# A state-space scan loop: two of sixteen blocks take their input through ScalarE and GpSimd, and the steps around the loop are placed anew

## The chip, the core and the metric

The kernel runs on one core of one Trainium2 chip. The metric is the time of one execution in microseconds of device time. The kernel before took 2898.57 us, the median of three runs (2897.48 to 2911.18). The profile shown in this document is of one further execution, which took 2914.13 us and whose profiled span is 2912.3 us.

## What is computed

The reference is a two-layer model on a tensor of 4 images, 256 channels and 32 x 32 pixels (1024 positions). Layer 0 holds four small state-space blocks ("mamba"), one for each group of 64 channels, then gates, depthwise convolutions, attention and a projection. Layer 1 is a second attention and a mixture of 16 experts. The change lies wholly in the state-space part, which for one image and one channel group is this:

```python
u = silu(causal_conv(u))                       # 128 inner channels, 1024 positions
dt = softplus(xdbc[..., :4] @ dtw.T + dtb)     # 128 x 1024
Bm, Cm = xdbc[..., 4:20], xdbc[..., 20:]       # 16 states, 1024 positions each
def selective_scan(u, dt, Bm, Cm, A, Dp):
    dA = exp(dt[..., None] * A)
    dBu = (dt * u)[..., None] * Bm[:, :, None, :]
    def step(h, inp):
        dA_t, dBu_t, C_t = inp
        h = dA_t * h + dBu_t
        return (h, einsum('bds,bs->bd', h, C_t))
    ...
    return ys + u * Dp
y = selective_scan(...) * silu(z) @ outw.T
```

## The kernel before

**Tiles.** An image and a channel group make one *group* `n` of the loop: 16 groups, image by image (`order`, four of them an image). A group has 128 inner channels with 16 states each, 2048 recurrences along 1024 positions. They are cut into `NJ` = 16 *blocks* of 8 channels x 16 states = 128 partitions x 1024 positions. The loop runs over `t` = 0 to 255 (`NBLK`) blocks; `n, j = t // 16, t % 16`. Every tile named below is 128 x 1024 float32.

**One block** is made by five engines:

- the DMA queue of SyncE (`fetch`, L869) spreads the 8 rows of `dt` over 128 partitions into `dA` (five buffers), and ScalarE (`decay`, L874) takes the exponential in place;
- TensorE (`select`, L881) multiplies a 0/1 matrix `pick` with `U`, three bfloat16 parts of dt*u, so that PSUM tile `dBu` (two buffers) holds dt*u on 128 partitions;
- VectorE multiplies `dBu` in PSUM by `B` (L940) and runs the recurrence `h = dA*h + dBu` (L943) into `hs` (six buffers);
- GpSimd multiplies `hs` by `C` (L944);
- TensorE sums over the states into `pY` (`add_up`, L892 for the first block and the last two, L899 for pairs of the others) and adds u * D (L905). `pY` has one buffer.

**The order of the work** is written out by hand: each engine works through its own queue in the order in which the loop body emits. Iteration `t` emits the multiply and the scan of block `t`, the C-multiply of `t`, `select(t + 2)`, `add_up(t - 3)`, `fetch(t + 4)`, `decay(t + 3)`, and then *front* steps of the coming group, which make its `u`, `dt`, `U`, `B` and `C`. The list at L526 to L529 gives each front step the `j` at which it is emitted (negative numbers are in the group before):

| step | engines and lines | j before | j after |
|---|---|---|---|
| `project(0..3)`, the convolution | TensorE L464 | -5, -4, -3, -2 | -4, -3, -3, -1 |
| `silu` | ScalarE L468 | -1 | -1 |
| `project_dt` | TensorE L475 | 0 | 0 |
| `exps` | ScalarE L480 to L483, four operations | 1 | 0 |
| `rest` | VectorE L486, GpSimd L487 | 3 | 3 |
| `log` | ScalarE L490 | 4 | 3 |
| `dt_out` | VectorE L493, DMA L495, GpSimd L496 | 5 | 5 |
| `part1`, `part2`, the bfloat16 parts | ScalarE L500, L505; GpSimd L501, L506 | 6, 7 | 6, 7 |
| `spread(0)`, `spread(1)`, B and C | TensorE L522, ScalarE L524 | 6, 7 | 6, 9 |
| `parts_out`, `turn` | DMA L510, L517 | 10, 12 | 11, 12 |

Behind the loop steps of the group just finished are emitted too: `gated` (ScalarE copies `pY` into `u`, L546), `times_gate` (GpSimd, L549, j = 4), `project_out` (TensorE, L559 and L560), `store` (ScalarE, L565), `gate` of the running group (TensorE L537, ScalarE L539), `module_gate` (TensorE L578 or L589, j = 5, in groups 5, 6, 7, 9, 10, 11, 13, 14, 15) and `module` (GpSimd L594, in groups 6, 7, 10, 11, 14, 15). All products of front and back steps share one PSUM tile, `mm` (`big()`).

**What waits for what around the change.** `select` of a block needs its PSUM buffer back from the scan two blocks earlier. The first `add_up` of a group needs `pY` back, that is `gated` of the group before. `dt_out` on VectorE needs `log` of ScalarE and the subtraction L487 of GpSimd. The scan needs an `hs` buffer that `add_up` has read.

Of the kernel before, what the change touches and what calls it, by code (L numbers as in the profile page):

```python
# [10 lines left out]
F32 = mybir.dt.float32  # L11
BF16 = mybir.dt.bfloat16
AF = mybir.ActivationFunctionType
ALU = mybir.AluOpType
# [3 lines left out]
B, C, HH, WW = 4, 256, 32, 32  # L18
N = HH * WW
NP = N + 2  # L20
P = 128
CT = C // P
NT = N // P
NB, DM, DIN, DS, DTR, K = 4, 64, 128, 16, 4, 4
# [352 lines left out]
def body(tc, g, out):  # L377
    nc = tc.nc
    act, mm = nc.scalar.activation, nc.tensor.matmul
    ts, tt, stt = nc.vector.tensor_scalar, nc.vector.tensor_tensor, nc.vector.scalar_tensor_tensor  # L380
    HALVES = (slice(0, 512), slice(512, 1024))
# [5 lines left out]
    with pool("const", 1) as cp, pool("dram", 1, space=bass.MemoryType.DRAM) as drp, contextlib.ExitStack() as late:  # L387
# [46 lines left out]
        with pool("mconst", 1) as mc, pool("front", 1) as fp, pool("dts", 2, space=bass.MemoryType.DRAM) as dsp, pool(  # L434
# [17 lines left out]
            def front(n):  # L452


                nb, b = order[n]
                rows_in, xb = block(nb, b)
                r = state[n] = {}

                def project(part):
                    if part == 0:  # L460
                        r["pu"] = big()
                    h = HALVES[part // 2]
                    for k in range(part % 2 * 2, part % 2 * 2 + 2):
                        mm(r["pu"][:, h], m_cu[rows_in, nb // 2, k], xb[:, k + h.start : k + h.stop], start=k == 0, stop=k == K - 1)  # L464

                def silu():
                    r["u"] = fp.tile([P, N], F32, tag="u", name="u", bufs=3)
                    act(r["u"], r["pu"], AF.Silu, bias=V("convb", nb), scale=1.0)  # L468

                def project_dt():
                    r["pdt"] = big()
                    for h in HALVES:
                        mm(r["pdt"][:, h], m_wdt[:, nb, :], r["u"][:, h], start=True, stop=True)  # L475

                def exps():
                    e = r["e"] = fp.tile([P, N], F32, tag="e", name="e")
                    dt = r["dt"] = fp.tile([P, N], F32, tag="dt", name="dt")
                    act(e, r["pdt"], AF.Abs, bias=V("dtb", nb), scale=1.0)  # L480
                    act(dt, r["pdt"], AF.Relu, bias=V("dtb", nb), scale=1.0)
                    act(e, e, AF.Exp, scale=-1.0)
                    act(r["pdt"], e, AF.Identity, bias=one, scale=1.0)  # L483

                def rest():
                    stt(r["e"], r["pdt"], -1.0, r["e"], ALU.add, ALU.subtract)  # L486
                    nc.gpsimd.tensor_tensor(r["dt"], r["dt"], r["e"], ALU.subtract)  # L487

                def log():
                    act(r["pdt"], r["pdt"], AF.Ln)  # L490

                def dt_out():
                    tt(r["dt"], r["dt"], r["pdt"], ALU.add)  # L493
                    r["ds"] = dsp.tile([NJ, DB, N], F32, tag="ds", name="ds")
                    nc.sync.dma_start(out=r["ds"].rearrange("j d n -> (j d) n"), in_=r["dt"])  # L495
                    nc.gpsimd.tensor_tensor(r["e"], r["dt"], r["u"], ALU.mult)  # L496

                def part1():
                    p = r["parts"] = fp.tile([P, 3, N], BF16, tag="parts", name="parts")
                    nc.scalar.copy(p[:, 0], r["e"])  # L500
                    nc.gpsimd.tensor_tensor(r["e"], r["e"], p[:, 0], ALU.subtract)  # L501

                def part2():
                    p = r["parts"]
                    nc.scalar.copy(p[:, 1], r["e"])  # L505
                    nc.gpsimd.tensor_tensor(p[:, 2], r["e"], p[:, 1], ALU.subtract)  # L506

                def parts_out():
                    dq = r["dq"] = dsp.tile([P, 3, N], BF16, tag="dq", name="dq")
                    nc.sync.dma_start(out=dq, in_=r["parts"])  # L510

                def turn():

                    dq = r["dq"]
                    U = r["U"] = fp.tile([96, 4, N], BF16, tag="U", name="U", bufs=2)
                    for q in range(3):
                        nc.sync.dma_start(out=U[32 * q : 32 * q + 32], in_=dq.rearrange("(t c) q n -> q c t n", c=32)[q])  # L517

                def spread(c):
                    p = big()  # L520
                    for h in HALVES:
                        mm(p[:, h], m_bc[:, nb, c * P : (c + 1) * P], r["u"][:, h], start=True, stop=True)  # L522
                    t = r["BC"[c]] = fp.tile([P, N], F32, tag=f"bc{c}", name=f"bc{c}", bufs=2)
                    nc.scalar.copy(t, p)  # L524

                return [(i - 5, lambda i=i: project(i)) for i in range(4)] + [  # L526
                    (-1, silu), (0, project_dt), (1, exps), (3, rest), (4, log), (5, dt_out), (6, part1),
                    (6, lambda: spread(0)), (7, part2), (7, lambda: spread(1)), (10, parts_out), (12, turn),
                ]  # L529

            def gate(n):
# [66 lines left out]
            with pool("scan", 6) as sp, pool("yps", 1, space=PSUM) as yps, pool("dps", 2, space=PSUM) as dps, pool("lnA", 1) as wp:  # L598
# [8 lines left out]
                add, pre.spare, pre.slack, pre.split = pre.add, (2, 3), 700, True  # L607
                xs = [[sp.tile([P, N], F32, tag="hs", name="hs") for k in range(CT)] for b in range(B - 1)]
                for b in range(B - 1, B):
                    t = wp.tile([P, CT, N], F32, tag=f"xs{b}", name=f"xs{b}")  # L610
                    xs.append([t[:, k] for k in range(CT)])
                    late_gate.append(t.rearrange("p k n -> p (k n)")[:96, 0:NP])
                convr = sp.tile([P, N], F32, tag="dA", name="dA", bufs=5).rearrange("p (t k d) -> p t k d", t=CT, k=K)
                roots = [sp.tile([P, N], F32, tag="dA", name="dA", bufs=5) for b in range(2)]
                roots += [wp.tile([P, N], F32, tag="r", name="r")] * 2
# [241 lines left out]

                dAs, dBus, hss = {}, {}, {}  # L860

                def which(t):

# [7 lines left out]
                def decay(t):  # L871
                    if t < NBLK:
                        c = order[t // NJ][0] * NJ + which(t)
                        act(dAs[t], dAs[t], AF.Exp, scale=aneg[:, c : c + 1])  # L874

                def select(t):
                    if t < NBLK:
                        j = which(t)
                        dBus[t] = dps.tile([P, N], F32, tag="dBu", name="dBu")
                        for h in HALVES:  # L880
                            mm(dBus[t][:, h], pick[:, j % 4], state[t // NJ]["U"][:, j // 4, h], start=True, stop=True)  # L881

                def add_up(t):
                    if not 0 <= t < NBLK:
                        return
                    r, p, j = state[t // NJ], t % NJ, which(t)
                    if p == 0:
                        r["pY"] = yps.tile([P, N], F32, tag="y", name="pY")
                    if not 2 <= p < 14:
                        hs = hss.pop(t)  # L890
                        for h in HALVES:
                            mm(r["pY"][:, h], strip[:, P - DB - j * DB : 2 * P - DB - j * DB], hs[:, h], start=p == 0, stop=p == NJ - 1)  # L892
                    elif p % 2:

                        two = {which(u): hss.pop(u) for u in (t - 1, t)}
                        for h in HALVES:
                            for c, hs in two.items():
                                q, i = c // 4, c % 4
                                mm(  # L899
                                    r["pY"][32 * q : 32 * q + 32, h], strip[:, P - DB - i * DB : P - i * DB + 32 - DB], hs[:, h],  # L900
                                    start=False, stop=False,
                                )
                    if p in (0, 1):
                        h = HALVES[p]
                        mm(r["pY"][:, h], ddiag[:, order[t // NJ][0]], r["u"][:, h], start=False, stop=False)  # L905

                fronts = [front(n) for n in range(1, len(order))]
# [26 lines left out]
                with tc.manual_schedule():  # L934
                    for t in range(NBLK + 4):
                        n, j = t // NJ, t % NJ
                        if t < NBLK:
                            r = state[n]
                            dBu = dBus.pop(t)
                            tt(dBu, dBu, r["B"], ALU.mult)  # L940

                            hs = hss[t] = sp.tile([P, N], F32, tag="hs", name="hs")
                            nc.vector.tensor_tensor_scan(hs, dAs.pop(t), dBu, 0.0, ALU.mult, ALU.add)  # L943
                            nc.gpsimd.tensor_tensor(hs, hs, r["C"], ALU.mult)  # L944
                        if j == 3 and n > 0:
                            gated(n - 1)
                        select(t + 2)
                        add_up(t - 3)
# [11 lines left out]
                            times_gate(n - 1)  # L960
                        last = n == len(order)
                        for i in range(2):
                            if n > 0 and j == (3 if last else 8 + i):
                                project_out(n - 1, i)
                        if n > 0 and j == (3 if last else 9):
                            store(n - 1)
                        if not last and j == 10:
                            gate(n)
                        if n > NB and j == 5 and n % NB > 0:
                            module_gate(n // NB - 1, n % NB - 1)  # L970
                        if n > NB and j == 8 and n % NB > 1:
                            module(n // NB - 1, n % NB - 2)


# [1103 lines left out]
```

## Time and profile before

| what | value |
|---|---|
| median of three runs | 2898.57 us |
| the profiled execution | 2914.13 us |
| its span | 2912.3 us |
| scan loop, first to last scan (L943) | 102.7 to 1068.1 us |
| TensorE busy over the span | 89% |
| VectorE | 69% |
| ScalarE | 53% |
| GpSimd | 44% |
| TensorE clock granted, mean | 0.947 |

The page of a profile lists busy time by engine, forty equal slices of the span, DMA queues, the chain of work that ended last and the costliest groups of instructions: after the bar come busy time in all, the mean duration of one in ns, and the idle time of the engine just before them with what ended most of it. The timeline lists instructions in order of time: start and duration in us, engine, line, operation; identical neighbours are merged, and a bracket gives the idle time before the row and what released it. The windows view gives the busy time of every engine in a stretch and the clock granted to TensorE in it (1.00 is full speed).

### The profile page before, as it was taken

How to read it: one execution, taken by the hardware profiler on the slowest of the kernel's cores; microseconds unless marked ns; L12 is line 12 of the kernel's file. 1: busy time of each engine (PE TensorE's matmuls, PEld its weight loads, DVE VectorE, ACT ScalarE, POOL GpSimd, SP SyncE). 2: the span in 40 equal slices, each digit the busy share in tenths (PEclk: the TensorE clock that was granted, in tenths of full speed). 3: DMA queues.
4: the chain of work that ended last, by engine and by line, in shares of the span. 5: the costliest groups of instructions: out<-in, count | busy, mean ns of one | idle time of the engine just before them, and what ended most of it. 6: DMA issues, size and time to landing. Idle time of an engine off the chain costs nothing. (4 is left out here: it accounts for less than half of the span.)

```text
span 2912.3 us, 38753 instructions
## 1 busy us (share of the span) xinstructions
PE 2582.6 (89%) x15252; PEld 1505.6 (52%) x15252; DVE 1999.3 (69%) x2260; ACT 1554.3 (53%) x2097; POOL 1281.2 (44%) x806
## 2 busy tenths in 40 slices
PE   6788888888888779999899899989799997899996
PEld 3322222222222225666556556554566676799996
DVE  5799999999999986867876895783655465111112
ACT  3666666766766635766855875783433332111111
POOL 0587778877888850000010010101234235666662
PEclk7799999999999989999999999999899997999998
DMA  3467667776677641001000000000000003655445
GB/s 141 119 175 176 173 163 177 184 179 173 171 176 192 169 137 41 5 9 33 5 1 27 19 1 12 20 1 15 1 8 16 8 15 97 196 134 136 111 111 174
DMA packets 95433, 269.57 MB, mean 93 GB/s; under 512 B 18695, under 2 KB 36727, under 8 KB 91921
## 3 DMA queue, kind: packets, MB, share of 16 engines
q1 hardware_dynamic: 66560, 202.52, 26.5%
q0 software_dynamic: 26512, 60.35, 8.1%
q10 hardware_dynamic: 2176, 4.19, 0.4%
q8 instruction: 121, 1.98, 0.3%
q14 instruction: 64, 0.52, 0.1%
HBM read 291.57 MB, written 42.80 MB: 115 GB/s over the span
## 5 line engine op out<-in xcount | busy, mean ns | idle before, releaser
L944 POOL TENSOR_TENSOR hs<-hs,bc 128x1024 f32<-128x1024 f32 x256 | 600.9, 2356 | 162.1 <-DVE hs L943 157.2
L943 DVE TENSOR_TENSOR_SCAN hs<-dA,dBu 128x1024 f32<-128x1024 f32 x256 | 585.3, 2286 | 38.9 <-PE pY L899 10.0
L1286 DVE TENSOR_REDUCE nm<-s 128x1 f32<-128x1024 f32 x256 | 302.8, 1218 | 100.7 <-PE s L1277 99.8
L874 ACT ACTIVATE dA<-dA,aneg 128x1024 f32<-128x1024 f32 x256 | 286.3, 1144 | 105.9 <-DMA dA<-ds 104.0
L1291 ACT ACTIVATE pr<-s,nm 128x1024 f32<-128x1024 f32 x256 | 285.5, 1118 | 82.0 <-DVE nm L1286 44.4
L940 DVE TENSOR_TENSOR dBu<-dBu,bc 128x1024 f32<-128x1024 f32 x256 | 309.8, 1210 | 11.1 <-PE dBu L881 11.0
L1305 PE MATMUL k<-const,pr 128*128 128x128 f32 x2048 | 282.8, 280 | 31.1 <-ACT pr L1291 20.0
L1355 POOL TENSOR_TENSOR b<-b 128x1024 f32<-128x1024 f32 (+1 forms) x15 | 29.6, 1973 | 633.7 <-ACT b L1351 633.7
L1305 PEld LDWEIGHTS k<-const,pr 128*128 128x128 f32 x2048 | 227.7, 142 | 149.2 <-issue 76.3
L881 PE MATMUL dBu<-U,pick 96*128 96x512 bf16 x512 | 161.1, 397 | 121.4 <-DVE hs L943 121.2
L1953 PE MATMUL s<-pT,b 128*128 128x128 f32 x1920 | 236.4, 280 | 8.2 <-DMA b<-we,intse 6.9
L1953 PEld LDWEIGHTS s<-pT,b 128*128 128x128 f32 x1920 | 231.5, 196 | 14.3 <-issue 6.3
L899 PE MATMUL pY<-hs,const 128*32 128x512 f32 x768 | 214.6, 686 | 0.0
L1957 DVE TENSOR_TENSOR pT<-pT,s 128x512 f32<-128x512 f32 x72 | 49.3, 684 | 230.3 <-ACT pT L1956 230.3
L1309 ACT COPY pT<-k 128x512 f32<-128x512 f32 x299 | 165.2, 592 | 57.8 <-PE k L1305 56.4
L881 PEld LDWEIGHTS <-pick 96*128 96x128 bf16 x512 | 39.9, 98 | 298.0 <-issue 172.5
L1277 PE MATMUL s<-b,b 32*128 32x512 f32 x512 | 177.1, 652 | 8.1 <-ACT pr L1291 8.0
L1309 DVE COPY pT<-k 128x512 f32<-128x512 f32 x213 | 140.1, 684 | 62.3 <-PE k L1305 60.1
L1277 PE MATMUL s<-b,qs 32*128 32x512 f32 x512 | 177.1, 652 | 0.0
L1325 PE MATMUL k<-pT,b 128*32 128x128 f32 x4096 | 140.0, 277 | 4.7 <-ACT pT L1309 2.2
L464 PE MATMUL mm<-xm,m_cu 64*128 64x512 f32 x240 | 124.9, 643 | 8.1 <-ACT sz L539 8.1
L892 PE MATMUL pY<-hs,const 128*128 128x512 f32 x256 | 122.9, 602 | 9.5 <-ACT u L546 6.3
(482 smaller groups left out, 4634.3 us busy)
## 6 DMA issues: line engine op xcount, KB each, us to landing
dA<-ds SPq DMA_DIRECT2D x256, 512.0 KB, 4.7
dq<-parts SPq DMA_DIRECT2D x15, 768.0 KB, 6.0
U<-dq SPq DMA_DIRECT2D x45, 256.0 KB, 6.2
ds<-dt SPq DMA_DIRECT2D x16, 512.0 KB, 3.0
b<-x SPq DMA_DIRECT2D x4, 1024.0 KB, 6.2
acc<-pr SPq DMA_DIRECT2D x8, 512.0 KB, 7.4
qs<-b SPq DMA_DIRECT2D x32, 128.0 KB, 2.2
xm<-x SPq DMA_DIRECT2D x4, 1024.0 KB, 5.1
```

Source lines behind the costliest of these rows:

```text
L874: act(dAs[t], dAs[t], AF.Exp, scale=aneg[:, c : c + 1])
L881: mm(dBus[t][:, h], pick[:, j % 4], state[t // NJ]["U"][:, j // 4, h], start=True, stop=True)
L899: mm(r["pY"][32 * q : 32 * q + 32, h], strip[:, P - DB - i * DB : P - i * DB + 32 - DB], hs[:, h], start=False, stop=False,)
L940: tt(dBu, dBu, r["B"], ALU.mult)
L943: nc.vector.tensor_tensor_scan(hs, dAs.pop(t), dBu, 0.0, ALU.mult, ALU.add)
L944: nc.gpsimd.tensor_tensor(hs, hs, r["C"], ALU.mult)
L1277: mm(S[i][:, HALVES[h]], q, kT[rr, HALVES[h]], start=True, stop=True)
L1286: "DVE", 1130, lambda i=i, u=u: nc.vector.tensor_reduce(nms[u], S[i], AX.X, ALU.max, negate=True),
L1291: "ACT", 1100, lambda i=i, u=u, hd=hd: act(prs[u % 4], S[i], AF.Exp, bias=nms[u], scale=1.0, accum_out=rss[b % 2][:, k, qt, hd : hd + 1]), ...
L1305: nc.tensor.transpose(bank.t[:, j * P : (j + 1) * P], prs[u][:, c0 : c0 + P], ident)
L1309: 470, 598, lambda dst=dst, bank=bank: nc.scalar.copy(dst, bank.t), lambda dst=dst, bank=bank: nc.vector.tensor_copy(dst, bank.t),
L1953: mm(p12[:, a, c], wbufs[w][:, o : o + P], xT[:, k], start=k == 0, stop=k == CT - 1)
```

## The change

For two blocks of a group, those with j = 2 and j = 6 (`early`, from block 22 on, 29 blocks in all), `dBu` no longer stays in PSUM. TensorE still selects dt*u, three blocks ahead and not two, into the PSUM buffer that the scan just left; ScalarE copies it to an SBUF tile `scaled`; GpSimd multiplies that tile by `B` in place; the scan reads it there, and VectorE's multiply is left out. The PSUM buffer is then used again by the `select` of the same iteration. The PSUM buffers are taken in turn by the blocks that are not early. `scaled` is cut from a tile that held an input of the stage before. The front steps, `gated`, `project_out`, `store`, `gate` and `module` get other places, as the diff says, and the two halves of u * D go with blocks 0 and 2 and not 0 and 1.

```diff
-                return [(i - 5, lambda i=i: project(i)) for i in range(4)] + [
-                    (-1, silu), (0, project_dt), (1, exps), (3, rest), (4, log), (5, dt_out), (6, part1),
-                    (6, lambda: spread(0)), (7, part2), (7, lambda: spread(1)), (10, parts_out), (12, turn),
+                return [(i, lambda k=k: project(k)) for k, i in enumerate((-4, -3, -3, -1))] + [
+                    (-1, silu), (0, project_dt), (0, exps), (3, rest), (3, log), (5, dt_out), (6, part1),
+                    (6, lambda: spread(0)), (7, part2), (9, lambda: spread(1)), (11, parts_out), (12, turn),
                 ]
...
-                    t = wp.tile([P, CT, N], F32, tag=f"xs{b}", name=f"xs{b}")
-                    xs.append([t[:, k] for k in range(CT)])
-                    late_gate.append(t.rearrange("p k n -> p (k n)")[:96, 0:NP])
+                    t = wp.tile([P, NP + N], F32, tag=f"xs{b}", name=f"xs{b}")
+                    xs.append([t[:, k * NP : k * NP + N] for k in range(CT)])
+                    late_gate.append(t[:96, 0:NP])
+                    scaled = t[:, NP:]
...
+                def early(t):
+                    return NJ + 3 <= t < NBLK and t % NJ in (2, 6)
+
                 def select(t):
-                    if t < NBLK:
+                    if t < NBLK and t not in dBus:
                         j = which(t)
-                        dBus[t] = dps.tile([P, N], F32, tag="dBu", name="dBu")
+                        place = first[turns[0] % 2]
                         for h in HALVES:
-                            mm(dBus[t][:, h], pick[:, j % 4], state[t // NJ]["U"][:, j // 4, h], start=True, stop=True)
+                            mm(place[:, h], pick[:, j % 4], state[t // NJ]["U"][:, j // 4, h], start=True, stop=True)
+                        if early(t):
+                            dBus[t] = scaled
+                            nc.scalar.copy(dBus[t], place)
+                            nc.gpsimd.tensor_tensor(dBus[t], dBus[t], state[t // NJ]["B"], ALU.mult)
+                        else:
+                            dBus[t] = place
+                            turns[0] += 1
...
-                    if p in (0, 1):
-                        h = HALVES[p]
+                    if p in (0, 2):
+                        h = HALVES[p // 2]
...
-                            tt(dBu, dBu, r["B"], ALU.mult)
+                            if not early(t):
+                                tt(dBu, dBu, r["B"], ALU.mult)
...
-                        if j == 3 and n > 0:
+                        if early(t + 3):
+                            select(t + 3)
+                        if n > 0 and j == (3 if n == len(order) else 4):
                             gated(n - 1)
                         select(t + 2)
...
-                            if n > 0 and j == (3 if last else 8 + i):
+                            if n > 0 and j == (3 if last else 8):
                                 project_out(n - 1, i)
-                        if n > 0 and j == (3 if last else 9):
+                        if n > 0 and j == (3 if last else 8):
                             store(n - 1)
-                        if not last and j == 10:
+                        if not last and j == 11:
                             gate(n)
...
-                        if n > NB and j == 8 and n % NB > 1:
+                        if n > NB and j == 10 and n % NB > 1:
                             module(n // NB - 1, n % NB - 2)
```

More of the change, by code (lines that the diff above doesn't have):

```diff
@@ L854, in first_front @@
                             add("ACT", 580, lambda c=c, H=H, bank=bank: nc.scalar.copy(r["BC"[c]][:, H], bank.t), (), [("bc", c, h)], bank, give=True)
-                dAs, dBus, hss = {}, {}, {}
+                dAs, dBus, hss, turns = {}, {}, {}, [0]
                 def which(t):
```

## The prediction

> **What bounds the kernel now.** I read the page first, then the windows view cut at the loop's groups, then the timeline of one group.
>
> ```profile
> span 2912.3 us, 38753 instructions
> ...
> L944 POOL TENSOR_TENSOR hs<-hs,bc 128x1024 f32<-128x1024 f32 x256 | 600.9, 2356 | 162.1 <-DVE hs L943 157.2
> L943 DVE TENSOR_TENSOR_SCAN hs<-dA,dBu 128x1024 f32<-128x1024 f32 x256 | 585.3, 2286 | 38.9 <-PE pY L899 10.0
> ...
> L940 DVE TENSOR_TENSOR dBu<-dBu,bc 128x1024 f32<-128x1024 f32 x256 | 309.8, 1210 | 11.1 <-PE dBu L881 11.0
> ```
>
> In the loop GpSimd waits for VectorE's scan (157.2 us), while VectorE, at 2.29 + 1.21 = 3.50 us a block, has hardly any idle time of its own. So the loop is bound by VectorE. How closely, the groups show (columns: length; busy time of PE, weight loads, DVE, ACT, POOL; granted clock):
>
> ```profile
> 477.80:536.50 58.70, 50.67 (x149) 16.29 (x148) 56.84 (x35) 41.80 (x39) 50.43 (x23) 1.00 0.72 179
> 595.10:656.70 61.60, 52.25 (x137) 15.68 (x136) 57.05 (x34) 38.45 (x36) 48.54 (x22) 0.89 0.66 171
> 656.70:715.40 58.70, 51.72 (x151) 16.75 (x150) 56.84 (x35) 39.89 (x37) 48.54 (x22) 1.00 0.71 179
> ```
>
> An undisturbed group is 58.7 us: 16 blocks at 3.54 us (start to start) plus 1.1 each for `rest` and `dt_out`. Groups 1 to 14 lie between 175.4 and 1012.3 us, 59.8 us each; the 1.1 us over 58.7 come with a lower TensorE clock. VectorE has 1.9 us of slack a group, TensorE 8, GpSimd 8 to 10. A gain on VectorE is thus soon met by two other engines.
>
> **What the change takes away.** 29 multiplies of 1.21 us leave VectorE: 35 us in all, 2.4 in a group. The instruction order of the changed program confirms 29 copies, 29 GpSimd multiplies, and no other new instruction.
>
> **What it adds to ScalarE and TensorE.** 29 PSUM copies on ScalarE at 1.01 us (nearest row: the copy L524 of the same shape). ScalarE is 42 of 58.7 us busy, so what counts is when. I walk the queues from the end of the scan of block 15 (time 0) to block 7 of the next group (block 23), with durations of the group at 536 us. Scans end at 3.54 (block 16), 7.08, 9.42 (block 18, without its multiply), 12.96 (block 19, j = 3), 17.6, 21.1 (block 21).
>
> Select 0.66, copy 1.71, select of 17 at 2.37 (wanted at 3.5: hidden), `project(3)` 4.3, `silu` 5.4, `project_dt` 8.0. Then ScalarE: `exps` 4.15 us (544.90 to 549.05) to 12.2, two `decay` of 1.1 to 14.4, the copy for block 22 to 15.4. Behind it stand `decay` 16.5, table load 17.8, Ln 18.8 and only then `gated` 19.8, since it went from j = 3 to 4. The first `add_up` of a group waits for `gated` because `pY` has one buffer. Before, that wait was 1.19 us (551.23 in the timeline); now TensorE has 3.8 us with nothing to do (16.1 to 19.85). Behind this wait are queued: `add_up` of block 16 (1.8 us), half of u * D (0.95), `add_up` of 17 (1.8), and the select of block 23 (0.6), which VectorE wants at 24.5. It comes at 25.05 at full clock.
>
> It won't be full clock:
>
> ```profile
> 536.10:539.50 3.40, 1.20 (x6) 0.34 (x7) 3.27 (x3) 3.36 (x4) 2.26 (x2) 1.00 0.65 154
> 539.50:542.90 3.40, 3.40 (x9) 0.53 (x5) 3.27 (x3) 1.94 (x2) 2.16 (x2) 0.50 0.69 157
> ...
> 539.33 3.49 PE L899 MATMUL pY<-hs,const 128*32 128x512 f32 x8
> ```
>
> A stretch of 3.4 us with TensorE 1.20 us busy is followed by one at half clock, in which eight matmuls take 3.49 us for 1.91. [...] The trace halves after a window that is one third busy; the changed program has 1.2 us of work between 13.0 and 19.85, so I take the trace: 1.5 to 4.9 us of half clock by the window's phase, 3.2 in the middle, 1.6 us of delay. Select of block 23 at 26.7, 2.2 us after VectorE wants it. From there nine blocks at 3.54 to the end of block 31: 31.9. A group is 58.6 us. The 2.4 us are given back almost whole.
>
> **What it adds to GpSimd.** 29 multiplies at 2.356 us (L944, same shape): 4.7 us a group, to 53.2 to 55.1. And the early scans now read `dA` and `dBu` both from SBUF; before, one input of every scan and multiply lay in PSUM. No scan of the trace does this next to GpSimd, but other VectorE operations do:
>
> ```profile
> 1471.70 2.36 POOL L1355 TENSOR_TENSOR b<-b 128x1024 f32<-128x1024 f32 x1 [5.29 <-ACT b L1351]
> 1473.56 1.58 DVE L1043 SCALAR_TENSOR_TENSOR b<-xm,vec,b 128x1024 f32<-128x1024 f32 x1
> ...
> 1971.74 5.30 POOL L1382 TENSOR_TENSOR b<-b,misc 128x1024 f32<-128x1024 f32 x2 [10.46 <-DVE misc L1378]
> 1972.82 2.37 DVE L1372 SCALAR_TENSOR_TENSOR b<-pr 128x1024 f32<-128x1024 f32 x1 [1.22 <-ACT pr L1369]
> ```
>
> L1043 (median 1.28 us) ends 1.08 after GpSimd's end at 1474.06; L1372 (1.22 alone) takes 2.37. They wait for the running GpSimd operation, and GpSimd's next one waits for them. By these rows alone the scan's price lies between 0 (scans exempt) and a whole GpSimd operation, 2.36 us, each. [...] Block 18 comes when GpSimd has just finished (C-multiplies of 15 and 16, the B-multiply between): 0.1 us. Block 22 comes at 22.3 inside the C-multiply of 20, and waits until 23.6: 1.3. It ends at 25.9, before the select of block 23 at 26.7, so this wait lies beside the other. If scans are exempt the group stays 58.6; the dearest case is 2.3 more. For GpSimd the two scans are 4.6 us of standing still, in all 57.8 us a group, 59.7 where `module` is in it: about VectorE's chain, and no slack.
>
> **The moved steps.** `module_gate` (1.84 us, two such in groups 5, 9, 13) now meets a late TensorE: the pair of 18 and 19 frees `hs` for block 24 0.45 us late in five groups, 2.3 in three, 9 us in all. `spread(1)` to j = 9, `gate` to 11, both halves of `project_out` to 8, u * D to blocks 0 and 2: the same matmuls; I find every select 1 us or more ahead, so nothing, and 2 us a group if half clock falls there. `parts_out` one block later: 6.0 us to land, then SP's queue goes on to `U` (6.2) and the `dA` loads behind; `U` is there 4 us before VectorE needs it. `exps` earlier hides behind `decay`; unhidden it is 4.15. The loop's start may move 3 us either way.
>
> **The sum.** 58.6 + 9/14 + 1.1 for the half clocks that were there before = 60.3 against 59.8: +0.6 in 14 groups, +8.4. Group 15, without front steps, keeps one scan's wait: -1.2. Together +7. The profiled execution (2914.1) lies 15.6 us above the median, as one of the three runs (2911.2) does; I put the difference on the median: 2906.
>
> **The rivals.**
> - *Exchange* (likeliest, 0.45): as summed, 2906; its own range 2886 to 2913.
> - *GpSimd lags* (0.35, slower). GpSimd needs 57.8 us, `module` adds 0.7 on average, and its waits for the bfloat16 casts, 1.2 a group before (17.8 us in the waits view of the loop), stay: 59.7, so it never catches up. Then block 18 too meets a running operation, 1.2 us on average, in front of the whole chain: 61.5 a group, +23; up to 62 if `dt_out` waits as well, whose subtraction on GpSimd is due at 21.25 when the scan ends at 21.1. So 2914 to 2931, centre 2921. It decides from a lag of 0.5 us at block 15 (60.8 a group). Against: the casts can hide behind C-multiplies in a late queue.
> - *The gain comes through* (0.20, faster): the half clock falls clear of block 23 and early scans don't wait. Select at 25.05, 57.0 + 0.6 a group: -31 with group 15 at most, 2868, centre 2877.
>
> **Numbers.** A measurement of this kernel tells 0.5% from no change, 14.5 us. Faster 0.2, same 0.45, slower 0.35. The range 2878 to 2929 leaves out half of the fast case and the end of the slow one.
>
> **What the next profile would show.** L940's successor 227 times; early scans well over 2.29 us next to GpSimd, and GpSimd multiplies up to 4.6 (the port; all at 2.29 refutes it); idle TensorE before the first `add_up` of a group, released by `gated`, some 3.8 us, with 0.5 clock behind it; block 23's multiply waiting for its select by some 2 us; GpSimd over 90% busy. I'm wrong if ScalarE reaches `gated` early, or if the groups fall to 57 us with these waits in them.

## The result, and the profile after

The changed kernel takes 2926.42 us, the median of five runs (2921.60 to 2929.95). The kernel before, with two more runs, has a median of 2908.14 us (2897.48 to 2912.04). The ratio is 1.0071, with a 95% interval of 1.0043 to 1.0099: slower by 0.7%, some 20 us by the ratio and 18 by the medians, where 7 were forecast. The ratio takes all runs of both kernels, so it is not quite that of the medians. The profiled execution of after took 2929.95 us, its span is 2927.8, 15.5 more than before.

The page of after first, the rows that answer to those of before:

```profile
span 2927.8 us, 38763 instructions
...
L957 POOL TENSOR_TENSOR hs<-hs,bc 128x1024 f32<-128x1024 f32 x256 | 651.3, 2560 | 74.8 <-DVE hs L956 74.0
L956 DVE TENSOR_TENSOR_SCAN hs<-dA,dBu 128x1024 f32<-128x1024 f32 x227 | 519.1, 2287 | 29.5 <-PE pY L911 4.0
...
L953 DVE TENSOR_TENSOR dBu<-dBu,bc 128x1024 f32<-128x1024 f32 x227 | 274.7, 1210 | 23.0 <-PE dBu L886 18.6
```

The multiply L953 is there 227 times, as it should be, and 35 us shorter in all (309.8 before). VectorE's waits for the select have grown (11.0 to 18.6 us). GpSimd waits for VectorE half as long as before (157.2 to 74.0 us), and its 256 multiplies by C, each the same work, take 651 us for 601: they stand still in between.

The windows view, groups 2, 3, 6 and 7 of after (columns as before: length; busy time of PE, weight loads, DVE, ACT, POOL; granted clock):

```profile
239.60:300.90 61.30, 51.77 (x140) 16.99 (x140) 55.71 (x32) 40.20 (x38) 56.03 (x24) 0.89 0.68 172
300.90:362.30 61.40, 51.73 (x140) 17.02 (x140) 55.75 (x32) 40.15 (x38) 56.10 (x24) 0.89 0.67 171
484.20:543.10 58.90, 50.42 (x144) 17.14 (x144) 55.53 (x32) 43.81 (x41) 58.02 (x25) 0.94 0.70 178
543.10:602.40 59.30, 50.02 (x144) 16.98 (x144) 55.92 (x33) 43.76 (x41) 57.99 (x25) 0.94 0.70 177
```

An undisturbed group now takes 58.9 us where it took 58.7. VectorE is busy 1 us less in it, GpSimd 56 us, or 58 with `module`. The clock is no longer 1.00 even in the best group. In time: groups 1 to 14 grew by 10.8 us (60.5 each, 59.8 before), group 0 by 2.5, group 15 by 1.0, the rest of the span by 1.2.

The timeline of group 7, around its first addition to `pY` (the scan of block 15 of the group before, L956, ended at 541.86):

```profile
560.67 1.02 ACT L546 COPY u<-pY 128x1024 f32<-128x1024 f32 x1
561.78 3.39 PE L904 MATMUL pY<-hs,const 128*128 128x512 f32 x4 [3.72 <-issue]
564.43 2.35 POOL L549 TENSOR_TENSOR u<-u,sz 128x1024 f32<-128x1024 f32 x1
565.22 3.71 DVE L956 TENSOR_TENSOR_SCAN hs<-dA,xs 128x1024 f32<-128x1024 f32 x1 [1.41 <-PE pY L904]
566.75 4.33 POOL L957 TENSOR_TENSOR hs<-hs,bc 128x1024 f32<-128x1024 f32 x1
567.59 0.60 PE L886 MATMUL dBu<-U,pick 96*128 96x512 bf16 x2
568.85 1.20 DVE L953 TENSOR_TENSOR dBu<-dBu,bc 128x1024 f32<-128x1024 f32 x1
```

TensorE stands idle 3.72 us until `gated` has emptied `pY`, and then runs the sum of block 0, four records, mostly at half clock (3.39 us; 1.88 in before). (Blocks 0 and 1 of a group are summed one by one, L904; the pairs, L911, begin with block 2.) So block 6's scan, at 565.22, first waited 1.41 us for an `hs` buffer that these products had to read. It then met GpSimd's multiply L549 and waited for its end at 566.78: the scan takes 3.71 us. The select of block 7 (567.59 + 0.60) is there before the scan has ended. GpSimd's multiply L957 from 566.75 stands still in turn (4.33 us).

Over the loop VectorE's two largest waits in after are these (what waited, for what: us in all, times, longest), where in before the scan waited for `pY` products 10.0 us in all and the multiply for the select 11.0:

```profile
DVE hs L956 <- PE pY L904: 21.3, 15, 1.8
DVE dBu L953 <- PE dBu L886: 16.0, 17, 1.6
```

The first is block 6's scan, once in each of groups 1 to 15. In six of groups 1 to 14 (1, 2, 3, 5, 9, 11) block 7's multiply then waits for its select too, by 0.5 to 0.9 us; in the other eight, as in group 7, the select is there first.

The durations of one line, L956 of after, from 160 to 1100 us (minimum, median, maximum in ns):

```profile
L956 DVE TENSOR_TENSOR_SCAN hs<-dA,dBu x216: 2285/2287/2289, 158.9 to 1079.7; 128x1024 f32<-128x1024 f32 x108
L956 DVE TENSOR_TENSOR_SCAN hs<-dA,xs x29: 2265/3337/4292, 200.8 to 1044.6; 128x1024 f32<-128x1024 f32 x29
```

With `dBu` in PSUM all scans take 2.287 us within 2 ns. With both inputs in SBUF they take 2.27 to 4.29 us: most at block 2 are at the lower end, all at block 6 take 3.2 or more. This wait of scan and GpSimd multiply for each other is what the prediction and the expectations call the port: a name for these times, since no run shows what in the chip makes them wait.

### The profile page after: what moved, and what is told of

It is laid out like the page before. It is cut to its first block, busy times and chain, and to the rows that moved or that the text cites. A ratio compares the mean times of both kernels' runs of the same rounds, so it can differ in the third digit from the quotient of the medians.

```text
span 2927.8 us, 38763 instructions
## 1 busy us (share of the span) xinstructions
PE 2585.7 (88%) x15252; PEld 1522.3 (52%) x15252; DVE 1986.2 (68%) x2231; ACT 1579.7 (54%) x2126; POOL 1387.2 (47%) x835
## 3 DMA queue, kind: packets, MB, share of 16 engines
q1 hardware_dynamic: 66560, 202.52, 26.2%
## 5 line engine op out<-in xcount | busy, mean ns | idle before, releaser
L957 POOL TENSOR_TENSOR hs<-hs,bc 128x1024 f32<-128x1024 f32 x256 | 651.3, 2560 | 74.8 <-DVE hs L956 74.0
L956 DVE TENSOR_TENSOR_SCAN hs<-dA,dBu 128x1024 f32<-128x1024 f32 x227 | 519.1, 2287 | 29.5 <-PE pY L911 4.0
L953 DVE TENSOR_TENSOR dBu<-dBu,bc 128x1024 f32<-128x1024 f32 x227 | 274.7, 1210 | 23.0 <-PE dBu L886 18.6
L1968 PEld LDWEIGHTS s<-pT,b 128*128 128x128 f32 x1920 | 232.9, 197 | 14.2 <-issue 7.0
L911 PE MATMUL pY<-hs,const 128*32 128x512 f32 x768 | 198.1, 640 | 0.0
L904 PE MATMUL pY<-hs,const 128*128 128x512 f32 x256 | 149.7, 715 | 53.7 <-issue 50.2
L1324 ACT COPY pT<-k 128x512 f32<-128x512 f32 x299 | 165.2, 592 | 57.8 <-PE k L1320 56.2
L1324 DVE COPY pT<-k 128x512 f32<-128x512 f32 x213 | 140.2, 684 | 62.1 <-PE k L1320 60.2
L1340 PEld LDWEIGHTS k<-pT,b 128*32 128x32 f32 x4096 | 105.1, 110 | 38.2 <-issue 22.7
```

Source lines behind the costliest of these rows:

```text
L1324: 470, 598, lambda dst=dst, bank=bank: nc.scalar.copy(dst, bank.t), lambda dst=dst, bank=bank: nc.vector.tensor_copy(dst, bank.t),
L1340: mm(bank.t[i * HD : (i + 1) * HD, 0:P], v[:, 4 * jh + j, hd * HD : (hd + 1) * HD], pTs[m][jh][:, i, j * P : (j + 1) * P], start=(jh, j) = ...
L1968: mm(p12[:, a, c], wbufs[w][:, o : o + P], xT[:, k], start=k == 0, stop=k == CT - 1)
```

## The experiments

The kernel before ran beside all of them: 2911.94 us beside the first four, 2909.15 beside the next, 2910.44 beside the last. Each ratio is to before, with its 95% interval, and compares all runs of both. "Copy of u" is `gated`; "none early" means that all products stay on VectorE.

**e1, the copy of u back at block 3.** Otherwise as after.

```diff
-                        if n > 0 and j == (3 if n == len(order) else 4):
+                        if n > 0 and j == 3:
                             gated(n - 1)
```

> The changed kernel with one step put back: gated (ScalarE's copy of pY) is emitted at j = 3 again, behind the early copy and in front of decay, table load and Ln. My theory: the late gated is what leaves TensorE idle for 3.8 us, brings the half clock, and holds back the hs buffer of block 6 and the select of block 7. Put back, gated ends at 16.4 us after the scan of block 15 and not at 19.8; the first sum ends at 18.3, long before the scan of block 6 wants its buffer (22.3), and the select of block 7 comes at 21.6 of 24.5. What stays is the wait of block 6 for GpSimd, some 1.3 us. Groups of about 58 us for 60.5: 30 us less than the changed kernel (20 to 38), 2890 to 2905. Rival, the port and GpSimd's load alone set the loop: at most 5 us less than the changed kernel, 2920 or more.

Measured: 2903.24 us, 0.9959 [0.9944, 0.9973], 23 us below after by the medians (1.1% by the ratios), in the range of the theory. The timeline of e1 at the same place of group 6 (block 15's scan ended at 472.31):

```profile
487.75 1.01 ACT L546 COPY u<-pY 128x1024 f32<-128x1024 f32 x1
488.85 3.21 PE L904 MATMUL pY<-hs,const 128*128 128x512 f32 x4
...
494.19 2.92 DVE L956 TENSOR_TENSOR_SCAN hs<-dA,xs 128x1024 f32<-128x1024 f32 x1
```

The copy comes 3.4 us earlier; TensorE had no idle time before the addition (no bracket), and block 6's scan has no wait for a buffer in front of it. It meets a GpSimd multiply near its end and loses 0.6 us. ScalarE's and GpSimd's work is the same as in after. One step of one instruction on ScalarE turns a loss of 0.7% into a gain of 0.4%.

**e2, the wait for GpSimd alone.** The kernel before, in which 29 products are written to an SBUF tile by VectorE itself, so that 29 scans read only SBUF. No work is moved to another engine; `scaled` is cut as in after.

```diff
-                            tt(dBu, dBu, r["B"], ALU.mult)
+                            if NJ + 3 <= t and j in (2, 6):
+                                tt(scaled, dBu, r["B"], ALU.mult)
+                                dBu = scaled
+                            else:
+                                tt(dBu, dBu, r["B"], ALU.mult)
```

> The kernel before, with one thing of the change alone: in the same 29 blocks VectorE's own multiply writes its product to an SBUF tile, so that the scan reads both inputs from SBUF. No copy on ScalarE, nothing more on GpSimd, no step moved. My theory: the scan waits for the GpSimd multiply that runs when it wants to start. In this kernel the C-multiply of the block before starts 0.1 us after its scan and the early scan would start 1.25 us later, so it waits about 1.15 us each time, 29 x 1.15 = 33 us (25 to 38): 2933 to 2945. GpSimd multiplies of up to 4.6 us beside it. [...]

Measured: 2936.11 us, 1.0078 [1.0062, 1.0095], +24. The durations of the scan's line in e2:

```profile
L948 DVE TENSOR_TENSOR_SCAN hs<-dA,dBu x215: 2286/2287/2289, 159.4 to 1090.9; 128x1024 f32<-128x1024 f32 x108
L948 DVE TENSOR_TENSOR_SCAN hs<-dA,xs x29: 3361/3441/4467, 197.0 to 1056.0; 128x1024 f32<-128x1024 f32 x29
```

Every one of the 29 takes at least 1.07 us longer, by where its input lies and nothing else. 29 x 1.15 = 33 us in the loop, of which the total shows 24. (At 1.21 us a multiply, a scan that always meets GpSimd so gives back what the early product saves.)

**e3, the early product with every other step at its old place.** Copy of u at block 3; the cut shows part of the edit, which puts back all the steps of the table, `project_out`, `store`, `gate`, `module` and u * D.

```diff
-                    (-1, silu), (0, project_dt), (0, exps), (3, rest), (3, log), (5, dt_out), (6, part1),
+                    (-1, silu), (0, project_dt), (1, exps), (3, rest), (4, log), (5, dt_out), (6, part1),
...
-                            if n > 0 and j == (3 if last else 8):
+                            if n > 0 and j == (3 if last else 8 + i):
```

> The early copies and GpSimd multiplies of the change alone, with every front and back step where it was before. My theory: gated is in front of Ln as before, so TensorE gets pY back at about 16.5 us after the scan of block 15 and no half clock hits the select of block 7. What stays is the wait of block 6 for GpSimd (1.3 us). Near the kernel with gated put back, 2890 to 2905. Rival, the copies and GpSimd multiplies are themselves what costs: 2920 or more.

Measured: 2929.56 us, 1.0054 [1.0037, 1.0071]: the expectation failed. The waits of VectorE in the loop (what waited, for what: us in all, times, longest):

```profile
DVE dBu L953 <- PE dBu L886: 22.3, 23, 6.3
DVE e L486 <- ACT mm L483: 13.1, 13, 1.0
```

`rest` (L486) waits 1.0 us for `exps` in 13 groups: behind the copy for the early block, `exps` at block 1 comes too late (0.2 us in all in before). On top, block 0 loses 0.5 to 1.5 us in 13 groups and block 9 0.4 to 2.2 in ten. So the early product needs the steps moved, as the change moved them; of these moves, the copy of u is the one that hurt.

**e4, the moved steps alone, none early.** `early` returns False; copy of u at block 4.

> The moved steps of the change alone, no early block. My theory: without the copy gated ends 17.5 us after the scan of block 15, TensorE's wait is 2.6 us, the scan of block 6 wants its buffer at 24.6 and has it at 19.4 to 21; the moved steps alone cost little: as before, -5 to +8 us, 2903 to 2916. Rival, the new places are the whole loss: 2920 or more.

Measured: 2921.62 us, 1.0036 [1.0021, 1.0051], +10, more than expected and on the side of the rival, "the new places are the whole loss". The waits of VectorE, then of TensorE, in the loop of e4:

```profile
DVE dBu L953 <- PE dBu L886: 21.4, 21, 2.2
...
PE pY L904 <- ACT u L546: 56.1, 13, 5.6
```

TensorE waits 4.3 us for the copy in each of 13 groups, and VectorE then waits for block 6's select. The late copy costs without any early block; that it alone of the new places does, e8 shows.

**e5, one early block.** e1, with block 2 early only (`t % NJ == 2`).

> The copy of u at its old place (block 3), and ScalarE and GpSimd make the product of block 2 of a group only; block 6 goes back to VectorE. In the run with both blocks and the old place of u, block 2's scan met no wait and block 6's waited 0.6 us for GpSimd. Theory A (each early block frees VectorE's 1.21 us multiply and gives back only the wait that its scan meets): block 6 was worth 1.21 - 0.6 = 0.6 us a group, so this one is 0.5 to 0.7 us a group slower than the run with both, 58.6 to 58.8 us a group, 2908 to 2916 us, within 0.3% of the kernel before. Theory B (the wait for the port and GpSimd's load at block 6 cost more than the trace shows there, since they make the multiplies by C late for blocks 7 to 10): as fast as the run with both, or faster by up to 8 us, 2895 to 2903 us. Reading: block 2's scan at about 2.27 us in most groups in both.

Measured: 2897.51 us, 0.9948 [0.9930, 0.9966], theory B's end: 5.7 us less than e1 by the medians, of which 2.8 lie between the two medians of before, and the intervals overlap. So block 6 early brings nothing on top of block 2 that these runs can tell. What it brings at block 7 goes again: by the traces eleven groups of e1 lose 1.3 us or more in front of block 11 (five in e5, 1.3 each), and group 5 takes 65.0 us (60.2). The timeline of e5 shows also why block 2 is worth its 1.4 us only at times, first in group 2, then in group 3:

```profile
236.35 3.53 PE L911 MATMUL pY<-hs,const 128*32 128x512 f32 x8
239.13 2.35 POOL L957 TENSOR_TENSOR hs<-hs,bc 128x1024 f32<-128x1024 f32 x1 [0.43 <-DVE hs L956]
240.00 3.62 DVE L956 TENSOR_TENSOR_SCAN hs<-dA,xs 128x1024 f32<-128x1024 f32 x1 [1.02 <-PE pY L911]
...
296.09 1.91 PE L911 MATMUL pY<-hs,const 128*32 128x512 f32 x8
298.68 2.27 DVE L956 TENSOR_TENSOR_SCAN hs<-dA,xs 128x1024 f32<-128x1024 f32 x1
298.90 4.20 POOL L957 TENSOR_TENSOR hs<-hs,bc 128x1024 f32<-128x1024 f32 x1 [0.42 <-DVE hs L956]
```

In group 3 the scan starts 0.22 us before GpSimd's multiply and takes 2.27 us; GpSimd waits (4.20). In group 2 the eight products in front ran at half clock (3.53 for 1.91), so the buffer came 1.02 late, GpSimd was first, and the scan lost 1.3 more: 2.4 us. The wait for the buffer (1.02 us) brought the wait for GpSimd (1.3) with it.

**e6 and e7, the next two stalls.** e6 is e1 with the halves of the output projection in blocks 8 and 9, `store` at 9, the second `spread` at 10; e7 also takes the zeroing of the route module's tile from group 5 to group 2.

```diff
-                            if n > 0 and j == (3 if last else 8):
+                            if n > 0 and j == (3 if last else 8 + i):
                                 project_out(n - 1, i)
...
+                        if t == 2 * NJ + 10:
+                            nc.gpsimd.memset(late_gate[0], 0.0)
```

> Both blocks early, u copied at block 3, and the two halves of the output projection again in blocks 8 and 9 (store at 9, the second spread at 10), since with both at 8 the select of block 11 stands behind four products at half clock and VectorE waits 1.2 to 1.5 us for it in about eleven groups. Theory A (that stall is TensorE's queue at block 8): gone or under 0.4 us, about 11 x 1.3 = 14 us less than with both halves at 8, less what another step loses, 2885 to 2897 us. Theory B (VectorE only waits there for what is late anyway, so the stall moves to block 12 or to the next group's copy of u): 2898 to 2906 us, with the same length of groups, 58.0 to 58.2 us.

> The run with the output projection in two blocks, and the zeroing of the route module's tile done once in group 2, where GpSimd keeps up, in place of group 5, where it waited behind multiplies by C that ran late and held ScalarE for 9 us. Theory A (the 65 us of group 5, 7 more than its neighbours, came of this one wait): group 5 falls to 58 to 60 us, 5 to 7 us less in all than the run before it in this list. Theory B (group 5 loses its time to the module's products and activations as such, as groups 9 and 13 do): group 5 stays above 62 us and the total within 3 us.

e6 measured 2911.29 us, 1.0014 [1.0004, 1.0024], slower than e1: neither theory. Block 10's stall is gone (3.61 us from its scan to the next, 4.69 in e1) and seven groups take 56.6 to 57.4 us, but groups 4, 7 and 11 take over 62. There block 2 is late, by the same pair of waits, and block 6 too, here in group 4 of e6:

```profile
349.56 3.33 DVE L956 TENSOR_TENSOR_SCAN hs<-dA,xs 128x1024 f32<-128x1024 f32 x1 [1.32 <-PE pY L911]
...
365.51 4.46 DVE L956 TENSOR_TENSOR_SCAN hs<-dA,xs 128x1024 f32<-128x1024 f32 x1
```

e7 measured 2904.36 us, 0.9983 [0.9974, 0.9993], 6.9 below e6, and group 5 fell from 65.6 to 58.8 us: theory A. In e1 that group shows what held it:

```profile
438.80 0.95 POOL L574 MEMSET xs<- 96x1026 f32 x1
439.79 1.01 ACT L581 ACTIVATE xs<-mm 4x1024 f32<-4x1024 f32 x1 [9.16 <-POOL xs L574]
...
447.43 1.23 DVE L953 TENSOR_TENSOR dBu<-dBu,bc 128x1024 f32<-128x1024 f32 x1 [8.28 <-PE dBu L886]
```

A memset of 0.95 us stood behind late multiplies on GpSimd, ScalarE behind it for 9.16 us, `mm` behind ScalarE, the select behind `mm`, VectorE behind the select for 8.28.

**e8, the moved steps, none early, copy of u at block 3.** e4 with e1's edit.

> The moved steps alone, no early block, and u copied at block 3 as before. With u copied at block 4 these steps measured +10 us. Theory A (the copy of u at block 4 alone costs the 10 us, the other moved steps nothing): 2900 to 2908 us, at most 0.2% from the kernel before; groups of 58.5 to 58.8 us; TensorE's wait ahead of the first addition to pY under 3 us. Theory B (the two halves of the output projection together at block 8 or the other moved steps cost too): 2911 to 2920 us, with a wait of VectorE for the select of block 11 of 1 us or more in most groups.

Measured: 2901.51 us, 0.9973 [0.9964, 0.9983]. Theory A for the copy's part: from e4 to e8 0.6%. But the other moves are not neutral, they gain 8 us on before. Its loop has groups of 59.7 us against 59.8: four stalls in front of block 14 of before, 10.6 us in all, are gone, and nearly as much is lost anew, most of it in front of blocks 9 and 11. Of the 11.3 us between the two profiled executions 6.5 lie ahead of the first scan (96.2 us, 102.7 in before), a stretch that takes 94.7 to 102.7 us in the profiles of the other runs. So the profiles, one execution each, don't show where the 8 us are; that stays open.

**e9 and e10, one early block with the stalls of e6 and e7 taken out.** e9 is e7, and e10 is e5 with e7's memset, block 2 early only in both.

> Only block 2 early, u copied at block 3, the two halves of the output projection in blocks 8 and 9, and the zeroing of the route module's tile in group 2. With one early block and both halves at block 8, six groups lost 1.4 us at block 10 and group 5 lost 2.9 us at block 8: theory A (these are TensorE's queue and GpSimd's) gives 2897.5 - 6 x 1.4 - 2.9 = 2886 us, 2882 to 2891. Theory B (each wait that goes shows another one behind it, as in the runs with two early blocks, where the halves apart took 1.1 us from block 10 and blocks 2 and 3 gave it back in four groups): 2893 to 2903 us, and block 2's scan waits for GpSimd in more groups than the four of the run with both halves at 8.

> Only block 2 early, u copied at block 3, both halves of the output projection at block 8, and the zeroing of the route module's tile in group 2 in place of group 5. Theory A (group 5's 2.9 us at block 8 come of that wait): 2.5 to 3.5 us less than with one early block alone, 2893 to 2896 us. Theory B (the stall is another's): 2896 to 2899 us, group 5 at 60 us.

e9 measured 2896.53 us, 0.9948 [0.9930, 0.9966], and e10 2895.89 us, 0.9955 [0.9939, 0.9971]: for e9 theory B, for e10 theory A by its time and by group 5 (57.3 us, 60.2 in e5), though 1.6 us is less than the runs can tell. e5, e9 and e10 can't be told apart, and all beat both kernels by 0.5% and 1.2%. The windows view of e10, its group 3:

```profile
293.00:350.30 57.30, 50.16 (x142) 16.55 (x142) 55.59 (x34) 39.10 (x36) 52.16 (x23) 0.94 0.72 184
```

57.3 us is 58.7 less the 1.4 that block 2 saves. GpSimd, at 52 us, has slack again.

**e11, the copy of u at block 5.** The suspected cost doubled.

```diff
-                        if n > 0 and j == (3 if n == len(order) else 4):
+                        if n > 0 and j == (3 if n == len(order) else 5):
...
-                        if 0 < n < len(order) and j == 4:
+                        if 0 < n < len(order) and j == 5:
                             times_gate(n - 1)
```

> The changed kernel with the copy of u one block later still (block 5 instead of 4, its multiply by the gate too): the suspected cost doubled. Theory A (the copy holds the first addition to pY, so block 6's scan gets its hs buffer late and then meets GpSimd's multiply): the copy starts some 3.5 to 4.5 us later, the first addition to pY with it, nothing hides it, and block 6's scan starts later by as much: 3 to 4.5 us in each of 14 or 15 groups, +42 to +65 us, 2968 to 2990. Theory B (GpSimd's lag sets the group and the copy's place only fills time): 2926 to 2940 us.

Measured: 2946.54 us, 1.0122 [1.0102, 1.0142], 20 us over after by the medians (0.5% by the ratios): theory A's chain, at less than half of its +42 to +65. The timeline of e11 (group 7, block 15's scan ended at 546.50):

```profile
567.77 0.99 ACT L546 COPY u<-pY 128x1024 f32<-128x1024 f32 x1
568.86 3.75 PE L904 MATMUL pY<-hs,const 128*128 128x512 f32 x4 [6.19 <-issue]
572.65 3.22 DVE L956 TENSOR_TENSOR_SCAN hs<-dA,xs 128x1024 f32<-128x1024 f32 x1 [4.20 <-PE pY L904]
```

The copy starts 2.5 us later than in after, not 3.5 to 4.5, and the whole chain with it: the wait for the buffer is 4.20 us, 1.41 in after. 1.6 us a group arrive at the group's length, because the stalls that after has at block 10 in three groups and at block 2 in two are not there, and the select of block 7 is less late.

**e12, the copy of u at block 4, block 2 early only.** After with `t % NJ == 2`.

> The changed kernel, u copied at block 4, with block 2 early only. Theory A (with u at block 4, block 6's scan waits for its hs buffer first and so meets GpSimd's multiply, two waits in series, which is the larger part of the loss; block 2 has neither): with block 6 on VectorE again the hs buffer is wanted 1.2 us later, 0.4 to 0.8 us a group less than with both, 2912 to 2920 us, still slower than before by 3 to 11 us because the copy at block 4 alone measured +10. Theory B (the early product as such costs time through GpSimd's load): midway between none early (2921.6) and both (2926.4), 2922 to 2926 us.

Measured: 2930.91 us, 1.0070 [1.0048, 1.0092], as slow as after. Both theories missed, 2912 to 2920 us and 2922 to 2926: giving block 6 back to VectorE does not help while the copy is late, and taking its multiply from GpSimd doesn't either. In 9 of 14 groups block 2 is late as well (2 in after), as here in group 7 of e12:

```profile
545.46 3.57 PE L911 MATMUL pY<-hs,const 128*32 128x512 f32 x8
548.00 1.15 ACT L875 ACTIVATE dA<-dA,aneg 128x1024 f32<-128x1024 f32 x1
548.27 2.35 POOL L957 TENSOR_TENSOR hs<-hs,bc 128x1024 f32<-128x1024 f32 x1 [0.43 <-DVE hs L956]
549.16 3.61 DVE L956 TENSOR_TENSOR_SCAN hs<-dA,xs 128x1024 f32<-128x1024 f32 x1 [1.03 <-ACT dA L875]
```

The bracket names ScalarE's exponential, which ended at 549.15. In after the same exponential is still running when the scan starts, so the scan doesn't need it. What ended last is the half-clock row at 545.46 + 3.57 = 549.03, as in e5.

## Why the forecast was right, and where it was not

Two tables hold the answer. First the ratios to before, all with the moved front steps:

| copy of u at block | none early | block 2 early | blocks 2 and 6 early |
|---|---|---|---|
| 3 | 0.9973 (e8) | 0.9948 (e5) | 0.9959 (e1) |
| 4 | 1.0036 (e4) | 1.0070 (e12) | 1.0071 (after) |
| 5 | | | 1.0122 (e11) |

Then the walk of the prediction as measured, in us from the end of block 15's scan, medians of groups 1 to 14 of one profile each:

| kernel | copy ends | TensorE idle before the addition | scan of block 6 starts | scan of block 7 starts |
|---|---|---|---|---|
| before | 14.2 | none | 24.6 | 28.1 |
| e8: 3, none | 15.3 | 0.6 | 24.7 | 28.2 |
| e5: 3, block 2 | 15.5 | 2.3 | 23.2 | 26.8 |
| e1: 3, both | 16.4 | 0.2 | 21.9 | 26.0 |
| e4: 4, none | 18.7 | 4.0 | 25.5 | 29.1 |
| e12: 4, block 2 (its 4 groups with block 2 in time) | 18.9 | 5.7 | 25.6 | 29.1 |
| e12, all groups | 20.6 | 4.9 | 27.3 | 30.8 |
| after: 4, both | 19.8 | 3.7 | 23.7 | 29.0 |
| e11: 5, both | 22.3 | 6.2 | 26.2 | 30.8 |

With the copy at block 3 each early block brings block 7's scan forward, by 1.4 and by 0.8 us. With the copy at block 4 the median start of that scan is 29.0 us or later, however many multiplies VectorE has been spared (28.3 in six groups of after whose select is in time). The copy sets it, through `pY` and what stands behind it on TensorE: in e4 and e12 the select of block 6, in after the `hs` buffer of block 6's scan. Moving the copy alone moves the time: from 4 back to 3 by 0.6% with none early (e4, e8) and by 1.1% with both (after, e1), from 4 to 5, with its multiply by the gate, by 0.5% the other way (e11). That is the prediction's "given back almost whole".

**The walk to the copy: right.** Forecast: `gated` ends at 19.8, the first addition at 19.85 after 3.8 us of idle TensorE. Measured 19.83, 19.93 and 3.7. Taking the trace's half clock was right: in all 14 groups, behind gaps of 3.3 to 3.8 us, the first addition took 3.3 to 3.75 us for 1.88, so 1.5 to 1.9 longer, where the sum has a delay of 1.6. That delay, and the 1.5 to 4.9 us of half clock "by the window's phase" in whose middle it lies, were my estimate from the one pair of stretches in before; no run shows that range.

**Block 6's two waits: a step that failed.** The prediction let the scan of block 6 start at 22.3, wait 1.3 us for GpSimd, end at 25.9, and said that "this wait lies beside the other", the select of block 7 at 26.7. The select was there at 26.3 to 26.8 in six groups, and in eight before it was wanted. But the scan also needed an `hs` buffer, which the delayed addition frees. That wait (0.6 to 1.8 us) stands in front of the one for GpSimd (0.9 to 1.5), not beside it, and the scan ended at 27.1, in those eight groups after the select. In the other six VectorE waited for the select on top, 0.5 to 0.9 us where 2.2 were forecast. I had followed the delay into the select queued behind it and not into the buffers that the same products free. The two failures, one wait too few and one too large, nearly cancel, which is luck: an undisturbed group came to 58.9 us for 58.6.

**The wait for GpSimd: right in its price.** That a scan waits as L1043 and L1372 did was my estimate; no scan of before shows it. e2 shows that scans are not exempt, 1.15 us each at the median (3.441 for 2.287). In after block 2 pays nothing in 12 of 14 groups (0.1 forecast), block 6 0.9 to 1.5 (1.3 forecast), 2.0 in group 15.

**GpSimd: 1.7 us a group too much, and the rival's mechanism absent.** 57.8 us a group were forecast and 59.7 with `module`; 56.1 and 58.0 were measured (groups 2 and 3, 6 and 7), as the two scans cost it 3.8 us of standing still for 4.6 and its multiply by `B` takes 2.00 us for 2.36. The rival "GpSimd lags" has the right total: 2926.42 lies in its 2914 to 2931, outside the 2886 to 2913 of the exchange, and only 2.6 us inside the whole range. But the lag at block 15 is 0.14 or 0.15 us in every group, where that rival needs 0.5; block 2 is late in two groups of after only; and e1, with the same work on GpSimd, is 1.1% faster. So a total on that rival's side came from the exchange, dearer than I made it: the mechanism was right, and that the range held owes something to the rival that was not there.

**The sum: too small by its ends.** Groups 1 to 14 were forecast at +8.4 us and measured +10.8; the three route groups lose 8.7 at blocks 7 to 9 for 9 forecast. The term of 1.1 us a group "for the half clocks that were there before" held in size and not in place, which is luck too. In before 10.6 of its 15 us are lost in front of block 14 in groups 1, 4, 8 and 13, as here in group 1, where eight products took 3.16 us for 1.91 at full clock:

```profile
226.35 3.16 PE L899 MATMUL pY<-hs,const 128*32 128x512 f32 x8
229.71 2.29 DVE L943 TENSOR_TENSOR_SCAN hs<-dA,dBu 128x1024 f32<-128x1024 f32 x1 [2.02 <-PE pY L899]
```

After loses nothing there. It loses about as much in other places: in front of block 11 in groups 1 to 3, at block 2 in groups 8 and 10, at the select of block 7. Group 15 was put at -1.2 and measured +1.0: it has the late copy too, which I left out because it has no front steps (with the copy at block 3, in e1, it is 3.4 us shorter than in after). Group 0 gave +2.5, inside the 3 us that I allowed for the loop's start, and the rest of the span +1.2, which was not in my sum. That makes 15.5 in the span for 7. I also took 2898.57 us for the kernel before, which five runs put at 2908.14: 9.6 of the 20.4 us between 2906 and 2926.42 are that.

**The moved steps: "so nothing" was wrong both ways.** But for the copy they gain 0.3% by e8, and by e3 the early product loses without them; I had looked only for harm in them. And some harm is there: with both halves of `project_out` at block 8 the select of block 11 comes 1.2 us late in groups 1 to 3 of after; in e6, where the halves are apart, that wait is gone.

## What to carry to other kernels

When work is taken off the bounding engine, write down for each instruction pushed back on another engine's queue whom it releases: here one PSUM copy, a block later, held the single buffer `pY`, and the gain was gone whatever VectorE was spared. Follow a late instruction into everything that it frees, buffers as well as the products queued behind it, and add waits of one instruction in series unless they are shown to run at once. Here an input moved from PSUM to SBUF was a cost by itself beside GpSimd's multiplies (e2: 1.07 us or more for each of 29 scans, +24 us in all), so try few such places, where GpSimd has slack: one early block of sixteen gave all the gain that the runs can tell.

## What the runs showed of the hardware that I had not expected

Whether the early scan or GpSimd's multiply started first was decided by tenths of a microsecond, and the scan paid only as the second: in e5 0.22 us ahead of GpSimd it took 2.27 us, 0.87 us behind it 3.62; in after the 12 that took 2.27 us began 0.23 ahead of the next multiply, and the 17 that took 3.2 or more began 0.2 to 1.3 behind one. In e5 that lag came behind eight products at half clock (3.53 us for 1.91), and groups with nearly the same instructions fall into two lengths: in e12 four of them take 59.6 to 60.2 us, six 61.3 to 61.7.

Idle gaps of TensorE of 3.3 to 6.2 us were paid for beyond their length: in groups 1 to 14 the clock was at half for 82 us in before, 140 in after and 149 in e11. In the clock records of before and after the granted clock changes on a grid of 3.41 us alone. Cut on that grid, these groups of after show the clock fall from full to half behind 20 stretches, 18 of them with TensorE busy for 1.64 us or less, two for 2.3 and 2.6; it stayed full behind 188, none of them under 1.72. It came back behind none under 2.79 us. In before 13 of 18 falls fit this (1.55 us or less), five behind 2.6 to 2.8 us don't. So in after none of these 20 stretches was idle: the half clock came behind 0.59 us of work or more, in 18 of them behind less than half of 3.41. Where on the grid a group's work falls differs from group to group; no run moved that alone. Nor was a seventh `hs` buffer tried, which might take block 6's first wait away.
